# Sparse attention by gathered lists: first h gather tied to the 29th k|v row, degrees taken from records, later lists held, half of the h statistics beside the sort

## The chip, the cores and the metric

The kernel runs on one core of one Trainium2 chip. The metric is the device time of one execution in microseconds (us), lower is better. A core has TensorE (PE, with its weight loads shown apart as PEld), VectorE (DVE), ScalarE (ACT), GpSimd (POOL) and SyncE (SP). SP, ACT and POOL also start transfers, each through a queue of its own that works in order; the transfers all run on the same 16 DMA engines.

## The reference

One graph-attention layer over N = 4096 nodes with D = 512 features and 8 heads of 64. All masks that the inputs set are ones, and the layer norms' scales are ones and biases zeros.

```python
hs = layer_norm(x);  ht = layer_norm(h_target)
q = (ht @ Wq + bq) / sqrt(64);  k = hs @ Wk + bk;  v = hs @ Wv + bv
logits = einsum('thd,shd->hts', q, k);  logits = where(adj != 0, logits, -1e30)
ctx = einsum('hts,shd->thd', softmax(logits), v)
ht = layer_norm(ht + ctx @ Wo + bo)
out = layer_norm(x + ht + gelu(ht @ W1) @ W2)
```

`adj` is a 4096 x 4096 matrix of int32 (64 MB), symmetric with ones on the diagonal, in which about one element in 256 is set. So a node has some 17 neighbours, at most 39 in the tiles that the kernel provides for.

## The kernel before

The kernel doesn't compute the dense logits. It turns each row of `adj` into a list of its neighbours, sorts the nodes by degree, and gathers only the neighbours' k and v. A dense version of everything stands behind a flag for inputs that do not fit, and is not run here.

**Projections** (`project`, L859.). x is read in 16 groups of two tiles of 128 rows, normalized, transposed on PE, and multiplied by Wk and Wv. Each tile gives one "k|v row" of 128 x 1024 floats: `source` (L913) runs eight matmuls into PSUM (two halves of four), ACT copies each half to SBUF (L925), and ACT's queue stores the row to the DRAM table `kvd` (L927). There are 32 such rows. The SBUF buffer is `tq` (three of them) while h rows are still to be read, and then three slots of the ring.

**The ring** `kv` has 17 slots of 128 x 1024 floats. Slots 0 to 6 hold quarters of `adj` rows in the first stage, slot 7 small tables, slots 8 to 10 rows of h_target, slot 11 the first records, slots 12 to 16 groups of x. Afterwards the whole ring takes gathered k|v rows.

**Lists** (`edges`, L709). `adj` is read in 32 tiles of 128 rows, each in four quarters of 512 KB (`quarter`, L701). ACT takes the sign of a quarter and sums it for the degree (L721, three buffers `sg`). DVE multiplies the signs by positions and takes the largest eight of each of five segments (L726, L728). After four quarters DVE decodes and merges these into the 24 first neighbours, and the rest goes to DRAM (`rest_d`, L759). Tiles up to NA + FILL = 21 use the ring's slots; the later ones use two buffers `a`.

**h statistics** (`moments`, L793). Each of the 32 tiles of h_target is read by SP and gets a bn_stats and a bn_aggr on DVE. `edges` takes one after each odd quarter, so the 32 are done within the 16 tiles of part A. Then `prepare` (L1365) raises all 32 variances to -0.5 on POOL (L1372) and writes the results into both parts' records.

**Sort** (`sort`, L800). The lists of part A (16 tiles) are sorted by degree: counts by matmul with ones, a scan and a rank (L845), and 16 indirect scatters on POOL that write the records (degree, target, row, statistics, 24 neighbours) to DRAM (L848). `fill` makes FILL = 5 further list tiles beside it. Part B is sorted in the same way after all lists.

**Attention** (`attention`, L1121). Tiles are taken in an order that pairs large and small degrees. `prefetch` (L962) loads a tile's records (seven buffers `rec`; the first two by POOL, the others by SP). `front` (L975) gathers the tile's rows of h_target by index into a `tq` buffer (L958, issued by POOL), normalizes them on ACT (L984), transposes, and projects q (L997, L999). Each gather of k|v rows is an indirect DMA of 128 rows of 4 KB, issued by POOL (L958); gathers run four groups of up to three ahead. For each group DVE multiplies k by q and reduces (L1180, L1184), ACT takes the exponential, and DVE (L1143) and ACT (L1163) multiply v, which PE adds up by transposes (L1151). `finish` (L1038) divides by the sums, projects with Wo and normalizes.

**Feed-forward** (`feed`, L1276). Pairs of tiles run through W1, gelu and W2 (L1291, L1294, L1300), are normalized and scattered to the output (L1268).

**What orders the work.** Streams written as Python generators are woven by the costs that they yield (`_weave`); a scheduler then places instructions on the engines, in the order of its own estimates, each engine keeping that order on the chip. The first weave has the projections, `prepare` (lists, sort, first fronts) and `fill`; the second has attention, feed-forward and `other_lists`, which starts at 40 and yields 1.5 times the lists' costs, and ends with the sort of part B. `verdict` (L1215) checks that no degree is above the number of neighbours that its tile provides for; it loads the degrees from the sorted records with two strided DMAs (L1225).

Of the kernel before, what the change touches and what calls it, by code (L numbers as in the profile page):

```python
# [443 lines left out]
def adj_resnorm_kernel(  # L444
# [85 lines left out]
    with tc.tile_pool(name="keep", bufs=1) as keep:  # L530
# [17 lines left out]
        with ExitStack() as late:  # L548
            lp = late.enter_context(tc.tile_pool(name="lists", bufs=1))
            kp = late.enter_context(tc.tile_pool(name="kv", bufs=1))  # L550
            sp = late.enter_context(tc.tile_pool(name="s2", bufs=2))
            ps = late.enter_context(tc.tile_pool(name="ps", bufs=1, space=PSUM))
            src = ExitStack()
            kvw = src.enter_context(tc.tile_pool(name="kvw", bufs=1))
            wp2 = late.enter_context(tc.tile_pool(name="s2w", bufs=1, side="right"))
# [141 lines left out]
            adjs = []  # L697
            DEEP = 7
            FILL = 5

            def quarter(i, h):  # L701
                if i < NA + FILL:
                    a = ring[:, (i * NQ + h) % DEEP, :].bitcast(I32)
                else:
                    a = lp.tile([P, QW], I32, name="a", bufs=2)
                nc.sync.dma_start(a, adj[i * P:(i + 1) * P, h * QW:(h + 1) * QW])
                return a

            def edges(i):  # L709
# [4 lines left out]
                for h in range(NQ):  # L714
# [16 lines left out]
                    if h % 2 and moms:  # L731
                        moments(moms.pop(0))
# [126 lines left out]
            def project(order, t=None):  # L859
# [53 lines left out]
                def source(n, j):  # L913
                    g, hT = order[n], state[n][1]
                    if asked or moms:
                        kvr = sp.tile([P, 2 * D], F32, name="tq", bufs=3)
                    else:

                        kvr = ring[:, 8 + (n * G + j) % 3, :]
                    for half, w in enumerate((wk, wv)):  # L920
# [4 lines left out]
                        nc.scalar.copy(kvr[:, half * D:(half + 1) * D], pkv)  # L925
                    r0 = 1 + (g * G + j) * P
# [28 lines left out]
            recs, tqs, h2Ts, done, ready = {}, {}, {}, set(), []  # L955
# [19 lines left out]
            def front(i):  # L975
# [4 lines left out]
                t = tq[:, :D]  # L980
                gather(t, h_target, rec[:, TGT:TGT + 1])
# [56 lines left out]
            def finish(i, p, cps, group, hs, mv):  # L1038


                rec, tq, cap = recs[i], tqs.pop(i), TILES[i][1]
                pm = sp.tile([P, MAXE, H], F32, name="pm", bufs=1)
# [68 lines left out]
            def first_fronts():  # L1111

                for i in range(EARLY):
                    prefetch(i)
                for i in range(EARLY):
# [5 lines left out]
            def attention():  # L1121
# [47 lines left out]
                for group in GROUPS:  # L1169
# [3 lines left out]
                    for i in group:  # L1173
                        cps = ps.tile([P, KC, P], F32, name="cps", bufs=2)
                        while k < len(SG) and SG[k][0] == i:
# [7 lines left out]
                            lg = sp.tile([P, S, H], F32, name="lg")  # L1183
                            nc.vector.tensor_reduce(lg[:, :n, :],  # L1184
# [30 lines left out]
            def verdict():  # L1215
# [8 lines left out]
                for (i0, n), rec in zip(PARTS, recs_d):  # L1224
                    nc.sync.dma_start(degs[:, i0:i0 + n, :], rec.rearrange("(n p) w -> p n w", p=P)  # L1225
                                      [:, :, DEG:DEG + 1])
                for i, cap in enumerate(CAPS_A + CAPS_B):
# [136 lines left out]

            def prepare():  # L1365
# [3 lines left out]
                while moms:  # L1369
                    moments(moms.pop(0))  # L1370
                nc.vector.tensor_scalar_add(veh, mvh[:, :, 1], EPS)
                nc.gpsimd.tensor_tensor(rsh, veh, mhalf, ALU.pow)  # L1372
                nc.vector.scalar_tensor_tensor(nmh, mvh[:, :, 0], -1.0, rsh, op0=ALU.mult,
                                               op1=ALU.mult)
                for R, (i0, n) in zip(Rs, PARTS):
                    Rf = R.bitcast(F32)
                    nc.vector.tensor_copy(Rf[:, :, RST], rsh[:, i0:i0 + n])
                    nc.vector.tensor_copy(Rf[:, :, RST + 1], nmh[:, i0:i0 + n])
# [8 lines left out]
            def fill():  # L1387
# [3 lines left out]
                yield 9.0  # L1391
                for cost in _take(ed, FILL * steps):
                    yield cost

# [4 lines left out]
            s2wa = late.enter_context(tc.tile_pool(name="s2wa", bufs=1))  # L1399
            psf = late.enter_context(tc.tile_pool(name="psf", bufs=2, space=PSUM))  # L1400

            def other_lists():
                for cost in ed:
                    yield 1.5 * cost
# [38 lines left out]
```

## Time and profile before

| | |
|---|---|
| median of four runs | 1885.31 us (1879.07 to 1887.89) |
| profiled execution, its own time | 1885.55 us |
| span of that execution | 1883.8 us |
| mean granted TensorE clock | 0.957 |

Busy time by stage of that execution (us; the share is the mean over the 16 DMA engines):

| stage | PE | DVE | ACT | POOL | clock | DMA share |
|---|---|---|---|---|---|---|
| 0 to 250 | 226.92 | 212.99 | 165.84 | 25.03 | 0.97 | 0.97 |
| 250 to 360 | 58.69 | 78.26 | 49.66 | 51.94 | 0.77 | 0.77 |
| 360 to 650 | 263.30 | 262.01 | 212.45 | 143.03 | 0.96 | 0.76 |
| 650 to 700 | 39.99 | 20.84 | 21.98 | 35.16 | 0.83 | 0.53 |
| 700 to 1700 | 952.81 | 804.76 | 724.23 | 595.23 | 0.98 | 0.73 |
| 1700 to 1884 | 164.61 | 56.37 | 64.74 | 32.43 | 0.96 | 0.18 |

The first row is projections and lists, the second the sort of part A and the beginning of the attention, the third attention, feed-forward and the remaining lists, the fourth the sort of part B, the others attention and feed-forward alone. In a row of the instruction view stand the start, the duration, engine, line, operation, what is written and read, the count, and in brackets the idle time before it with what ended that. A busy PE can still be slowed by its clock. An idle engine costs something only where others wait for it.

### The profile page before, as it was taken

The numbers are of one execution on the slowest core, as the hardware profiler recorded it, in microseconds if no ns is written. First come the engines' busy times: TensorE is split into PE (matmuls) and PEld (weight loads), VectorE is DVE, ScalarE is ACT, GpSimd is POOL, SyncE is SP. The second block draws the span as 40 slices with busy tenths as digits, with TensorE's granted clock in tenths as the row PEclk, the third lists the DMA queues.
The fourth block names the chain that finished last, engine by engine and source line by source line (L and its number), as shares of the span: only waits on it lengthen the run. The fifth ranks groups of instructions, "written<-read, shape, count | busy, mean of one in ns | idle before, by whom it ended". The sixth has DMA issues, their size and how long they took to land. (4 is left out here: it accounts for less than half of the span.)

```text
span 1883.8 us, 22937 instructions
## 1 busy us (share of the span) xinstructions
PE 1706.3 (91%) x7030; PEld 1100.0 (58%) x7030; DVE 1435.2 (76%) x2595; ACT 1238.9 (66%) x3131; POOL 882.8 (47%) x804
## 2 busy tenths in 40 slices
PE   7989883688899989999999989999999999999995
PEld 3444431456566646766666656666666666666664
DVE  6989876899898737777878889889877768787400
ACT  5766644577786737776777767777767667777411
POOL 1000144545545465656666676655555545555101
PEclk9999996798999989999999999999999999999998
DMA  9999968978777646777778778767677767766000
GB/s 337 370 385 368 353 192 304 359 266 286 286 268 254 207 152 220 266 244 259 253 253 276 264 267 282 269 229 253 222 236 235 251 210 237 238 218 224 23 1 24
DMA packets 147757, 463.28 MB, mean 246 GB/s; under 512 B 24468, under 2 KB 29160, under 8 KB 147624
## 3 DMA queue, kind: packets, MB, share of 16 engines
q0 software_dynamic: 95696, 342.19, 53.4%
q1 hardware_dynamic: 45168, 98.54, 14.7%
q10 hardware_dynamic: 6760, 20.98, 2.8%
q8 instruction: 58, 0.95, 0.2%
q14 instruction: 75, 0.61, 0.1%
HBM read 430.76 MB, written 30.89 MB: 245 GB/s over the span
## 5 line engine op out<-in xcount | busy, mean ns | idle before, releaser
L958 POOL DMA_INDIRECT kv<-kvd,rec x603 | 685.1, 1136 | 523.2 <-PE cps L1151 240.9
L1291 PE MATMUL pf<-h2T,w 128*128 128x256 f32 (+1 forms) x2176 | 475.5, 370 | 5.1 <-issue 4.3
L1300 PE MATMUL po<-w,gt 128*128 128x512 f32 x1024 | 470.6, 601 | 0.0
L1180 DVE TENSOR_TENSOR kv<-kv,tq 128x1536 f32<-128x1536 f32 (+2 forms) x211 | 352.0, 1677 | 114.1 <-DMA kv<-kvd,rec 94.2
L1291 PEld LDWEIGHTS pf<-h2T,w 128*128 128x128 f32 x2176 | 390.4, 192 | 71.1 <-issue 26.2
L1163 ACT ACTIVATE kv<-kv,pa 128x64 f32<-128x64 f32 x1520 | 391.4, 336 | 4.6 <-ACT pa L1160 0.9
L1184 DVE TENSOR_REDUCE lg<-kv 128x24 f32<-128x1536 f32 (+2 forms) x211 | 350.6, 1669 | 2.4 <-ACT xt L1264 0.5
L1151 PE MATMUL cps<-ident,kv 128*128 128x128 f32 x2008 | 267.2, 281 | 61.3 <-DVE kv L1143 38.7
L1151 PEld LDWEIGHTS cps<-ident,kv 128*128 128x128 f32 x2008 | 239.6, 145 | 137.2 <-issue 61.1
L1300 PEld LDWEIGHTS po<-w,gt 128*128 128x128 f32 x1024 | 188.7, 194 | 190.0 <-issue 189.4
L1143 DVE TENSOR_TENSOR kv<-kv,p 128x1024 f32<-128x1024 f32 (+1 forms) x211 | 249.6, 1191 | 46.5 <-ACT p L1188 37.8
L681 POOL TENSOR_TENSOR n_rs<-n_ve,mhalf 128x2 f32<-128x2 f32 (+1 forms) x50 | 43.3, 867 | 323.8 <-DVE n_ve L674 152.1
L1294 ACT ACT_TABLE_LOAD x108 | 138.6, 1283 | 1.6
L923 PE MATMUL pq<-wk,h2T 128*128 128x512 f32 x256 | 125.2, 634 | 11.0 <-ACT h2T L908 5.9
L728 DVE MAX8 cand<-sg 128x8 uint16<-128x103 uint16 (+1 forms) x640 | 131.5, 253 | 1.8 <-DVE gid L749 0.8
L721 ACT ACTIVATE sg<-kv 128x1024 uint8<-128x1024 int32 x84 | 88.7, 1058 | 65.3 <-DMA kv<-in_adj_dram 34.8
L1294 ACT ACTIVATE gt<-pf 128x512 f32<-128x512 f32 x128 | 76.4, 597 | 80.0 <-PE pf L1291 63.3
L997 PE MATMUL t<-wq,tq 128*128 128x512 f32 x256 | 117.9, 603 | 10.6 <-ACT tq L991 8.3
L923 PE MATMUL pq<-wv,h2T 128*128 128x512 f32 x256 | 117.7, 602 | 4.8 <-ACT kv L925 3.0
L1073 PE MATMUL t<-wo,rb 128*128 128x512 f32 x256 | 120.0, 613 | 1.4 <-DVE rb L1063 1.4
L1188 ACT ACTIVATE p<-lg 128x24 f32<-128x24 f32 (+2 forms) x179 | 33.6, 188 | 91.8 <-DVE lg L1184 64.5
L923 PEld LDWEIGHTS pq<-wk,h2T 128*128 128x128 f32 x256 | 50.6, 205 | 72.8 <-issue 54.9
(171 smaller groups left out, 1607.9 us busy)
## 6 DMA issues: line engine op xcount, KB each, us to landing
kv<-in_adj_dram SPq DMA_DIRECT2D x84, 512.0 KB
a<-in_adj_dram SPq DMA_DIRECT2D x44, 512.0 KB
kvd<-tq ACTq DMA_DIRECT2D x24, 512.0 KB
kv<-kvd,rec POOLq DMA_INDIRECT x603
kv<-in_L_gnn_h_target_dram SPq DMA_DIRECT2D x32, 256.0 KB
kv<-in_x_dram SPq DMA_DIRECT2D x15, 512.0 KB
w<-in_L_gnn_W_dram SPq DMA_DIRECT2D x6, 1024.0 KB
rest_d<-gid SPq DMA_DIRECT2D x32, 160.0 KB
```

The lines of the kernel that those rows point to most:

```text
L728: nc.vector.max(cand[:, h * SQ + s, :], wd[:, w0:w1])
L923: nc.tensor.matmul(pkv, hT[:, kc, j * P:(j + 1) * P], w[:, kc, :], start=kc == 0, stop=kc == KC - 1)
L958: nc.gpsimd.indirect_dma_start(out=dst, out_offset=None, in_=table[:, :], in_offset=bass.IndirectOffsetOnAxis(ap=idx, axis=0))
L1073: nc.tensor.matmul(pa, ct[:, c, :], wo[:, c, :], start=False, stop=c == KC - 1, skip_group_check=True)
L1143: nc.vector.tensor_tensor(v4, v4, p[:, j0:j0 + m, :].unsqueeze(3) .to_broadcast([P, m, H, HD]), ALU.mult)
L1151: nc.tensor.matmul(cps[:, c, :], kv[:, j, D + c * P:D + (c + 1) * P], ident, is_transpose=True, start=j0 + j == 0 and c == 0, stop=j0 + n ...
L1163: nc.scalar.mul(v, v, pa[:, hd:hd + 1])
L1180: nc.vector.tensor_tensor(kv[:, :n, :D], kv[:, :n, :D], tq[:, :D].unsqueeze(1).to_broadcast([P, n, D]), ALU.mult)
L1184: nc.vector.tensor_reduce(lg[:, :n, :], kv[:, :n, :D].rearrange("p j (h d) -> p j h d", h=H), AX.X, ALU.add)
L1291: nc.tensor.matmul(pf[:, k, :], w1[(f0 + k) // KC][:, kc, (f0 + k) % KC * P:((f0 + k) % KC + 1) * P], h2T[:, kc, :w], start=kc == 0, stop= ...
L1294: nc.scalar.activation(gt, pf, AF.Gelu_apprx_tanh)
L1300: nc.tensor.matmul(po[j], gt[:, k, j * P:(j + 1) * P], w2[(f0 + k) // KC][:, (f0 + k) % KC, :], start=False, stop=f0 + k == FC - 1, skip_g ...
```

## The change

- *h statistics.* In the first 16 list tiles one statistic is taken per tile (after the second quarter), from the 17th on three. `norms(part)` raises the 16 variances of one part and writes them to its records; part A's stands before the sort, part B's at the end of `fill`. FILL is 6 instead of 5, and `fill` begins at 6 instead of 9.
- *k|v rows.* The rows of the first 14 groups go through `tq`; the last four go through ring slots 13 to 15 instead of 8 to 10, which still hold h.
- *First h gather.* The first fronts are begun in the order of the weave only after the 29th k|v row; a one-column copy on ACT from that row into the gather's destination makes the gather wait for it.
- *Later lists.* The first two adjacency quarters into `a` that are asked for once a group's logits exist get a one-column copy on ACT from the newest logits first, and so wait for them.
- *Degrees.* `finish` copies the degree of its tile from the record in SBUF with one POOL instruction; the two loads from DRAM go. The check then compares in the tiles' order.
- *Pace.* `other_lists` yields 2.0 times the lists' costs.
- The pool stack `late` is renamed `last`; `late` is now the list that holds the 29th row.

```diff
@@ quarter, edges
             else:
                 a = lp.tile([P, QW], I32, name="a", bufs=2)
+                if logits and len(held_back) < 2:
+                    held_back.append(i)
+                    nc.scalar.copy(a.bitcast(F32)[:, 0:1], logits[-1])
             nc.sync.dma_start(a, adj[i * P:(i + 1) * P, h * QW:(h + 1) * QW])
...
-                    if h % 2 and moms:
+                    if (h == 1 or i >= NA and h != 2) and moms:
                         moments(moms.pop(0))
...
-            FILL = 5
+            FILL = 6
@@ source
-                    if asked or moms:
+                    if n < NG - 2:
                         kvr = sp.tile([P, 2 * D], F32, name="tq", bufs=3)
                     else:
-                        kvr = ring[:, 8 + (n * G + j) % 3, :]
+                        kvr = ring[:, 13 + (n * G + j) % 3, :]
...
+                    if n == 14 and j == 0:
+                        late.append(kvr)
@@ front, finish, first_fronts
                 t = tq[:, :D]
+                if i < EARLY:
+                    nc.scalar.copy(t[:, 0:1], late[0][:, 0:1])
                 gather(t, h_target, rec[:, TGT:TGT + 1])
...
                 rec, tq, cap = recs[i], tqs.pop(i), TILES[i][1]
+                nc.gpsimd.tensor_copy(degs[:, i, :], rec[:, DEG:DEG + 1])
...
                     prefetch(i)
+                while not late:
+                    yield None
@@ attention, verdict
                             lg = sp.tile([P, S, H], F32, name="lg")
+                            logits[:] = [lg[:, 0, 0:1]]
...
-                for (i0, n), rec in zip(PARTS, recs_d):
-                    nc.sync.dma_start(degs[:, i0:i0 + n, :], rec.rearrange("(n p) w -> p n w", p=P)
-                                      [:, :, DEG:DEG + 1])
-                for i, cap in enumerate(CAPS_A + CAPS_B):
+                for i, (_, cap) in enumerate(TILES):
@@ prepare, fill, other_lists
+            def norms(part):
+                i0, n = PARTS[part]
+                while moms and moms[0] < i0 + n:
+                    moments(moms.pop(0))
+                me = slice(i0, i0 + n)
+                nc.vector.tensor_scalar_add(veh[:, me], mvh[:, me, 1], EPS)
+                nc.gpsimd.tensor_tensor(rsh[:, me], veh[:, me], mhalf[:, me], ALU.pow)
+                nc.vector.scalar_tensor_tensor(nmh[:, me], mvh[:, me, 0], -1.0, rsh[:, me],
+                                               op0=ALU.mult, op1=ALU.mult)
+                Rf = Rs[part].bitcast(F32)
+                nc.vector.tensor_copy(Rf[:, :, RST], rsh[:, me])
+                nc.vector.tensor_copy(Rf[:, :, RST + 1], nmh[:, me])
...
                 ready.append("lists")
-                while moms:
-                    moments(moms.pop(0))
-                nc.vector.tensor_scalar_add(veh, mvh[:, :, 1], EPS)
-                nc.gpsimd.tensor_tensor(rsh, veh, mhalf, ALU.pow)
...
+                norms(0)
...
-                yield 9.0
+                yield 6.0
                 for cost in _take(ed, FILL * steps):
                     yield cost
+                norms(1)
...
-                    yield 1.5 * cost
+                    yield 2.0 * cost
```

## The prediction

> **What bounds the kernel now.** I read four views in this order: the busy times of the engines, the windows by stage, the instructions in order of time on POOL, ACT and DVE around the two places where the windows show PE idle, and the DMA queues of one such place.
>
> The busy times say that PE has the least slack, DVE the next least:
>
> ```profile
> PE 1706.3 (91%) x7030; PEld 1100.0 (58%) x7030; DVE 1435.2 (76%) x2595; ACT 1238.9 (66%) x3131; POOL 882.8 (47%) x804
> ```
>
> PE is idle for 1883.8 - 1706.3 = 177.5 us. The windows show where (window, then PE, PE loads, DVE, ACT, POOL busy us, granted clock, DMA share, GB/s):
>
> ```profile
> 200.00:250.00 50.00, 44.40 (x117) 20.44 (x116) 42.30 (x180) 31.08 (x59) 10.78 (x7) 0.93 0.91 341
> 250.00:300.00 50.00, 37.92 (x93) 16.86 (x92) 31.48 (x130) 25.12 (x49) 17.30 (x19) 0.93 0.54 161
> 300.00:320.00 20.00, 2.59 (x7) 0.80 (x5) 11.37 (x38) 6.26 (x14) 11.86 (x12) 0.67 0.88 324
> 320.00:340.00 20.00, 5.64 (x24) 4.84 (x24) 17.02 (x25) 8.96 (x35) 12.63 (x9) 0.50 1.03 406
> 340.00:360.00 20.00, 12.54 (x58) 9.52 (x59) 18.39 (x19) 9.32 (x36) 10.14 (x10) 0.72 0.96 381
> 650.00:700.00 50.00, 39.99 (x147) 23.87 (x146) 20.84 (x22) 21.98 (x57) 35.16 (x34) 0.83 0.53 161
> ```
>
> Between 250 and 360 PE loses 12.1 + 17.4 + 14.4 + 7.5 = 51.4 us, between 650 and 700 another 10.0. From 700 to 1700 PE is 95% busy. From 360 to 650 it loses 27 of 290 us while DVE is 90% busy: there the remaining lists and the attention share DVE. So the change is worth what it does in the hand-over from projections to attention, in the lists-beside-attention stage, and at the second sort near 650.
>
> The hand-over on POOL (last scatter, first and last early gather, first k|v gather), then on ACT:
>
> ```profile
> 263.38 0.99 POOL L848 DMA_INDIRECT rec<-kv,ranki  x1 [0.31 <-issue]
> 269.42 1.02 POOL L958 DMA_INDIRECT tq<-in_L_gnn_h_target_dram,rec  x1 [2.11 <-DMA rec<-rec]
> 274.80 0.94 POOL L958 DMA_INDIRECT xt<-in_x_dram,rec  x1 [0.30 <-issue]
> 304.15 0.94 POOL L958 DMA_INDIRECT kv<-kvd,rec  x1 [28.41 <-DMA a<-in_adj_dram]
> ```
>
> ```profile
> 262.79 1.06 ACT L721 ACTIVATE sg<-kv 128x1024 uint8<-128x1024 int32 x1 [7.17 <-issue]
> ...
> 273.00 0.81 ACT L984 ACTIVATE tq<-tq,rec 128x512 f32<-128x512 f32 x1 [4.08 <-DMA tq<-in_L_gnn_h_target_dram,rec]
> ...
> 283.20 1.06 ACT L721 ACTIVATE sg<-a 128x1024 uint8<-128x1024 int32 x1 [3.99 <-DMA a<-in_adj_dram]
> ...
> 295.38 1.06 ACT L721 ACTIVATE sg<-a 128x1024 uint8<-128x1024 int32 x1 [2.00 <-DMA a<-in_adj_dram]
> ...
> 297.03 0.33 ACTq L927 DMA_DIRECT2D kvd<-kv  x1
> ```
>
> The reader is to see that the k|v gathers wait 28.4 us on POOL, and that the 32nd k|v row is stored at 297.03 only because ACT, which works in order, stood 7.2 us ("issue" in the row; in the program that sign waits for DVE to free its buffer), 4.1 us for the first h gather and 6 us for adjacency quarters with copies of finished rows behind. And on DVE a pause ahead of the sort, the first product and a starved one at the second sort:
>
> ```profile
> 208.68 0.19 DVE L1373 SCALAR_TENSOR_TENSOR kv<-kv 128x32 f32<-128x32 f32 x1 [5.55 <-POOL kv L1372]
> ...
> 315.54 1.76 DVE L1180 TENSOR_TENSOR kv<-kv,tq 128x1536 f32<-128x1536 f32 x1 [5.54 <-DMA kv<-kvd,rec]
> ...
> 688.73 1.76 DVE L1180 TENSOR_TENSOR kv<-kv,tq 128x1536 f32<-128x1536 f32 x1 [13.62 <-DMA kv<-kvd,rec]
> ```
>
> **The change part by part.** The sum is made against the profiled execution's own 1885.55 us (span 1883.8), which stands 0.2 us above the median of the four runs, 1885.31. Positions come from the order in which the two programs' instructions stand on each engine.
>
> *Half of the h statistics beside the sort.* Two statistics take 1.28 us and their two aggregates 0.30 (rows at 209.10 and 210.29), so 0.79 each. Ahead of the degree sum (212.1) 14 of them go: 11.1 us. The power pause halves: POOL took 5.43 us for 32 columns and 0.58 for one, so 16 take about 2.9, minus 2.6. If DVE alone set the time the degree sum would come 13.7 us sooner; but ACT waits 18 us for adjacency quarters between 100 and 250, and its order ties the lists to PE's rows, of which only one fewer stands ahead (two halves of 3.43 and its share of transposes, 7.4 us). I take the mean, 10.6. Between degree sum and ranks the new order puts 8 statistics (6.3), two more quarters (1.3 each) and one more list end (3.8): plus 12.7. So the ranks come about 2 us later than 243.7; between 1 us sooner and 5 later by these two readings.
>
> *POOL behind the scatters.* The 16 scatters (20.3 us) stay. Ahead of the first h gather now stand both x gathers (2 x 1.25) and three copies of a degree. No copy on POOL is in the trace; I bound it by DVE's smallest, 0.17, and POOL's one-column power, 0.58, and take 0.58, the same engine: 1.7. The third copy also waits for a record that SP loads, 3.3 us of issue after the scatters, which the x gathers cover. With the ranks' 2 us the h gather starts at 275.6 instead of 269.4. The tie to the 29th row adds nothing: that row's first half was copied at 254, before any record. The second power (2.9) stands ahead of the k|v gathers, but DVE asks for it near 280, well before 295. All 32 copies are at most 18.6 us on an engine that is idle for 1001 us, so they are no term by their length. The Trainium skill, page "GPSIMD Engine Reference", section 3.1, speaks against putting them there: elementwise work on that engine costs about twice DVE's time. An estimate from that page and DVE's 0.17 would be 32 x 0.34 = 10.9 us, less than the bound by the row, and the sum would be the same.
>
> *The last rows.* In ACT's order the scale that waits for the h gather still stands ahead of the 30th row's copy, which moves from 273.7 to about 280. But from there to the last store ACT has only three signs of quarters (seven before), all of quarters loaded before the scatters, so the 3.99 + 0.74 + 0.56 + 2.00 us of waits for adjacency go. From 280: the 30th row is whole at 285, both halves of the 31st at 287, PE needs 3.6 us for each half of the 32nd (5.8 at the low clock, as 288.87 shows). The store comes at 294.8, minus 2 us. Bounds: minus 12, if DVE's slow stretch from 252 to 268 (8 us busy of 16) does not come back; plus 5, if the ranks are 5 late and the last waits stay.
>
> *Later lists held.* From the first k|v gather to the first product pass 11.4 us, with four quarters (2 MB) in flight. Without them the nearest row is the h gather, 3.6 us from start to use; the third gather starts 3.5 us after the first; with double the bytes I allow 4, together 7.5, minus 4 us (bounds 0 and minus 4). Held back are four quarters and one list end, 4 x 1.25 + 3.8 = 8.8 us of DVE. By the 41st product (593 us before) both orders have done the same list work since the first product, so the 8.8 us fall after 600, where DVE has 29 us free between 650 and 700 and 12 in the next 50: cost 0, at most 8.8 if that cover is gone. The four one-column copies that ACT gains for the tie and the hold cost 0.17 each, as its gate of the last weights does. What SP has queued behind a held quarter: later quarters, the writes of rest and the later records; DVE's lists wait for the first, nobody early for the others.
>
> *Lists at 2.0 instead of 1.5.* The 27 us that PE loses from 360 to 650 shrink with less list work per time; 10 lists over a third more time. I take minus 2 (0 to minus 8, about a third of 27).
>
> *The second sort.* Its 16 scatters stood almost in a row: no k|v gather from 662.8 to 684.5, and DVE starved 13.6 us. Now 8 scatters run, then k|v gathers stand between the rest: the longest gap is about 10 us, so DVE's wait should fall to 2 or 3. PE lost 10 us in that window, and part of it is slow issue from 678 to 694 that follows scatters in both orders. I take minus 5 (minus 10 to plus 3).
>
> *Degrees from records.* Two loads go from SP. In the DMA queues from 252 to 268 the first is the bulk of this row:
>
> ```profile
> q1 hardware_dynamic: 2087, 0.01, 7.4%
> ```
>
> 7.4% of 16 us is 1.2 us of DMA, while the engines were otherwise nearly idle; SP waits for the scatters with the records anyway. I take 0. The Trainium skill, page "DMA: Bandwidth & Descriptors", Rules for kernel authors, says that a strided last dimension becomes one descriptor per element, which the packet count agrees with; a rule for a gain, which this row prices at 1 us at best.
>
> Sum: -2 - 4 + 0 - 2 - 5 + 0 = -13, so 1885.55 - 13 = 1872.5, said as 1872.
>
> **The rivals.**
> 1. Slower: a degree copy holds POOL. 25 copies stand between k|v gathers, and each waits for a record that SP loads behind adjacency quarters; four of these kept SP from 411 to 468, 14 us each. Between an out scatter, which frees the record's place, and its copy POOL has 8 gathers, 10 us. A record 14 us late holds POOL about 4 us, for each of the 8 tiles whose lists are still open; PE and DVE then starve as at 688. From the fourth such hold on it eats the 13 us; five or six, 20 to 24 us, end at 1892 to 1896. Against it: records 7 to 9 were issued within 5 us of their out scatter.
> 2. No change: PE makes up nothing, because after 360 it is bound by DVE and the held 8.8 us come back: -13 + 8.8 + 2 for the pacing is -2, 1883 (1880 to 1888).
> 3. More: the ranks come early (the 13.7 us in full) and DVE's slow stretch misses ACT. Last store near 285: -12 - 4 - 4 - 8 = -28 at most, 1857; I put it at 1862. For it: DMA ran at 0.99 to 1.02 between 50 and 200, and 14 h rows, 3.7 MB, leave that stretch.
>
> **How the numbers follow.** Forecast 0.42 (1866 to 1879), rival 3 0.20, rival 2 0.17, rival 1 0.21. A measurement of this kernel tells about 0.3%, 5.7 us, from no change. Faster: 0.42 and 0.20; rival 2 is mostly within: 0.16; slower 0.22. The range goes from 1856, rival 3's end, to 1893, at the lower part of rival 1, and leaves out about 0.15.
>
> **What would show it.** Right: first k|v gather near 302, first product near 309, no quarter landing between them, the DVE wait near the second sort under 5 us, PE loss from 250 to 360 about 45 us. Wrong: POOL idle ahead of a degree copy for several us; the h gather past 280; DVE over 95% busy with PE idle after 650; or a first product after 315.

## The result and the profile after

The changed kernel takes 1891.1 us (median of 48 runs, 1881.6 to 1897.3) against 1885.7 us for the kernel before (75 runs, 1878.2 to 1891.2): the ratio is 1.0028, with a 95% interval of 1.0021 to 1.0035. The forecast was 1872 us, so the change went the other way, by 5 us up instead of 13 down.

The profiled execution of the changed kernel took 1887.6 us (span 1885.7), 2.05 us more than that of the kernel before. The busy times of the engines:

```profile
PE 1704.4 (90%) x7030; PEld 1103.0 (58%) x7030; DVE 1433.7 (76%) x2597; ACT 1225.7 (65%) x3127; POOL 886.7 (47%) x837
```

PE, DVE and ACT are busy less in all than before (by 1.9, 1.5 and 13.2 us), POOL with its 32 copies 3.9 us more. What changed is where PE waits. The windows by stage of the kernel before (columns as in the prediction: window, then PE, PE loads, DVE, ACT, POOL busy us, granted clock, DMA share, GB/s):

```profile
0.00:250.00 250.00, 226.92 (x593) 106.05 (x594) 212.99 (x907) 165.84 (x304) 25.03 (x40) 0.97 0.97 361
250.00:360.00 110.00, 58.69 (x180) 32.02 (x179) 78.26 (x209) 49.66 (x132) 51.94 (x49) 0.77 0.77 275
360.00:650.00 290.00, 263.30 (x1236) 181.91 (x1235) 262.01 (x513) 212.45 (x558) 143.03 (x129) 0.96 0.76 264
650.00:900.00 250.00, 238.12 (x1073) 161.81 (x1072) 171.59 (x170) 163.29 (x437) 151.19 (x140) 0.97 0.70 231
900.00:1400.00 500.00, 469.69 (x2063) 318.79 (x2062) 417.89 (x426) 366.48 (x998) 313.02 (x268) 0.97 0.75 254
```

The same windows of the changed kernel:

```profile
0.00:250.00 250.00, 223.11 (x594) 103.86 (x595) 217.31 (x926) 167.96 (x311) 24.02 (x41) 0.98 0.99 365
250.00:360.00 110.00, 67.42 (x218) 39.30 (x217) 69.47 (x169) 46.95 (x138) 62.26 (x64) 0.77 0.70 256
360.00:650.00 290.00, 259.56 (x1185) 177.86 (x1185) 260.25 (x530) 211.48 (x546) 131.61 (x124) 0.95 0.76 267
650.00:900.00 250.00, 227.77 (x1020) 156.79 (x1019) 165.27 (x167) 147.90 (x406) 148.32 (x139) 0.95 0.64 217
900.00:1400.00 500.00, 476.04 (x2120) 324.82 (x2119) 426.77 (x433) 373.83 (x1024) 316.69 (x284) 0.99 0.77 261
```

The idle time of PE is the window's length less its first busy figure:

| stage | PE idle before, us | after | difference | the prediction's steps |
|---|---|---|---|---|
| 0 to 250 | 23.1 | 26.9 | +3.8 | none |
| 250 to 360 | 51.3 | 42.6 | -8.7 | -2 (last rows) and -4 (hold) |
| 360 to 650 | 26.7 | 30.4 | +3.7 | -2 (pace), 0 (deferred work) |
| 650 to 900 | 11.9 | 22.2 | +10.3 | -5 (second sort) |
| 900 to 1400 | 30.3 | 24.0 | -6.3 | none |

The hand-over came out as well as foreseen, or better. In the instructions of POOL in order of time, the first k|v gather starts at 294.12 instead of 304.15:

```profile
294.12 1.03 POOL L964 DMA_INDIRECT kv<-kvd,rec  x1 [17.34 <-DMA kvd<-kv]
```

In those of DVE, the first product starts at 303.30 instead of 315.54:

```profile
303.30 1.76 DVE L1192 TENSOR_TENSOR kv<-kv,tq 128x1536 f32<-128x1536 f32 x1 [4.07 <-DMA kv<-kvd,rec]
```

Followed gather by gather (the first is number 0, so that n gathers stand ahead of the n-th), the lead is spent early. The 20th k|v gather starts 15 us sooner than before (322.8 against 338.2), the 40th 9 us, the 60th 4, the 80th 4 later (489.2 against 485.3). From there to the 140th it swings between 4 us sooner and 6 later. Then comes the second sort. In the kernel before its 16 scatters ran from 656 to 679; here, on POOL, they run from 722.90 to 758.87. First, last and one in the middle:

```profile
722.90 1.02 POOL L852 DMA_INDIRECT rec<-R,ranki  x1 [0.30 <-issue]
...
744.32 1.72 POOL L852 DMA_INDIRECT rec<-R,ranki  x1 [0.30 <-issue]
...
758.87 1.01 POOL L852 DMA_INDIRECT rec<-R,ranki  x1 [0.30 <-issue]
```

DVE, in order of time, waits for k|v gathers beside them in two pieces, and once more near 870:

```profile
743.39 1.76 DVE L1192 TENSOR_TENSOR kv<-kv,tq 128x1536 f32<-128x1536 f32 x1 [5.06 <-DMA kv<-kvd,rec]
761.58 1.76 DVE L1192 TENSOR_TENSOR kv<-kv,tq 128x1536 f32<-128x1536 f32 x1 [8.88 <-DMA kv<-kvd,rec]
...
870.89 0.69 DVE L1192 TENSOR_TENSOR kv<-kv,tq 128x512 f32<-128x512 f32 x1 [6.61 <-DMA kv<-kvd,rec]
```

The kernel before has, behind its one wait of 13.62 us, a second one:

```profile
700.81 1.76 DVE L1180 TENSOR_TENSOR kv<-kv,tq 128x1536 f32<-128x1536 f32 x1 [6.05 <-DMA kv<-kvd,rec]
```

DVE's waits of over 3 us for k|v gathers in this stage come to 20.6 us here and to 19.7 there, so they are not the difference. PE now has two long pauses; the kernel before has none of over 2 us in this stage, and loses its 10 us at the sort in many short ones:

```profile
769.99 1.12 PE L997 MATMUL t<-ident,tq 128*128 128x128 f32 x4 [8.36 <-ACT h L1087]
880.76 6.32 PE L1006 MATMUL t<-wq,tq 128*128 128x512 f32 x8 [8.63 <-issue]
```

The first pause follows the scatters, the second comes some 110 us behind the last of them. In windows of 50 us, the kernel before:

```profile
850.00:900.00 50.00, 48.57 (x235) 34.04 (x234) 36.50 (x36) 34.09 (x93) 35.59 (x31) 1.00 0.77 267
```

The changed kernel:

```profile
700.00:750.00 50.00, 47.38 (x212) 32.83 (x211) 35.00 (x42) 26.55 (x75) 32.75 (x30) 0.97 0.52 169
750.00:800.00 50.00, 41.01 (x184) 28.02 (x182) 30.79 (x30) 26.79 (x80) 34.77 (x32) 0.90 0.67 223
850.00:900.00 50.00, 41.37 (x179) 28.13 (x178) 28.65 (x30) 26.63 (x72) 30.50 (x29) 0.90 0.66 231
```

So at the sort PE loses 9.0 us (11.6 with the 50 us ahead), where the kernel before lost 10.0 from 650 to 700. Another 8.6 go from 850 to 900, where the kernel before lost 1.4.

The 220th gather is 6 us late, as the 140th was, with one sort behind both kernels. The 240th, behind the second pause, is 17 us late (917.9 against 900.5); the stage from 900 to 1400 gives that back by the 380th (1196.1 against 1196.2). The last gather is 2 us late, and so is the end.

### The profile page after: what moved, and what is told of

Its sections match the earlier page's. It is cut to its first block, busy times and chain, and to the rows that moved or that the text cites. A ratio compares the mean times of both kernels' runs of the same rounds, so it can differ in the third digit from the quotient of the medians.

```text
span 1885.7 us, 23007 instructions
## 1 busy us (share of the span) xinstructions
PE 1704.4 (90%) x7030; PEld 1103.0 (58%) x7030; DVE 1433.7 (76%) x2597; ACT 1225.7 (65%) x3127; POOL 886.7 (47%) x837
## 3 DMA queue, kind: packets, MB, share of 16 engines
q1 hardware_dynamic: 41040, 98.52, 14.6%
## 5 line engine op out<-in xcount | busy, mean ns | idle before, releaser
L1163 PE MATMUL cps<-ident,kv 128*128 128x128 f32 x2008 | 267.7, 281 | 40.5 <-DVE kv L1155 29.2
L1155 DVE TENSOR_TENSOR kv<-kv,p 128x1024 f32<-128x1024 f32 (+1 forms) x211 | 249.7, 1191 | 44.9 <-ACT p L1201 40.7
L681 POOL TENSOR_TENSOR n_rs<-n_ve,mhalf 128x2 f32<-128x2 f32 (+1 forms) x50 | 38.0, 759 | 321.3 <-DVE n_ve L674 172.3
L1006 PE MATMUL t<-wq,tq 128*128 128x512 f32 x256 | 125.8, 637 | 26.5 <-ACT tq L1000 16.4
L725 ACT ACTIVATE sg<-kv 128x1024 uint8<-128x1024 int32 x88 | 93.0, 1060 | 74.4 <-DVE cand L732 34.8
L927 PE MATMUL pq<-wk,h2T 128*128 128x512 f32 x256 | 121.3, 616 | 9.8 <-ACT h2T L912 5.5
L1006 PEld LDWEIGHTS t<-wq,tq 128*128 128x128 f32 x256 | 50.8, 204 | 86.1 <-issue 64.4
```

Of the source, the lines that this page charges most:

```text
L927: nc.tensor.matmul(pkv, hT[:, kc, j * P:(j + 1) * P], w[:, kc, :], start=kc == 0, stop=kc == KC - 1)
L1006: nc.tensor.matmul(pq, hT[:, kc, :], wq[:, kc, :], start=kc == 0, stop=kc == KC - 1)
L1155: nc.vector.tensor_tensor(v4, v4, p[:, j0:j0 + m, :].unsqueeze(3) .to_broadcast([P, m, H, HD]), ALU.mult)
L1163: nc.tensor.matmul(cps[:, c, :], kv[:, j, D + c * P:D + (c + 1) * P], ident, is_transpose=True, start=j0 + j == 0 and c == 0, stop=j0 + n ...
```

## The experiments

Three theories were set against each other at first. P: the pace of 2.0 does the harm, through the place of the second sort. C: the degree copies hold POOL. H: the held list work gives back the gain of the hand-over. The parts other than pace, hold and copies (half of the statistics beside the sort, six lists beside the projections instead of five, the tie, the ring places) are called the hand-over's parts below.

All results in one table. "Place" is the number of k|v gathers that stand on POOL, in the order of the program, ahead of the second sort's first scatter; PE idle is from the windows of each profiled execution.

| run | parts of the change in it | place | PE idle 360 to 900, us | ratio to before (95%) |
|---|---|---|---|---|
| before | none | 142 | 38.6 | 1 |
| after | all | 165 | 52.7 | 1.0028 (1.0021 to 1.0035) |
| e1 | all, pace 1.5 | 127 | 53.9 | 1.0035 (1.0016 to 1.0054) |
| e2 | all but the hold | 165 | 49.0 | 1.0021 (1.0003 to 1.0039) |
| e11 | the same again | 165 | 44.7 | 1.0016 (0.9994 to 1.0038) |
| e3 | all but the copies | 165 | 52.3 | 1.0027 (1.0012 to 1.0042) |
| e4 | hand-over | 127 | 40.5 | 0.9983 (0.9968 to 0.9997) |
| e16 | the same again | 127 | 39.8 | 0.9984 (0.9968 to 1.0001) |
| e5 | hand-over, hold | 127 | 50.9 | 1.0033 (1.0016 to 1.0050) |
| e6 | hand-over, pace 2.0 | 165 | 45.9 | 0.9984 (0.9966 to 1.0002) |
| e12 | the same again | 165 | 48.4 | 1.0007 (0.9992 to 1.0023) |
| e7 | hand-over, copies | 127 | 39.9 | 0.9995 (0.9979 to 1.0010) |
| e8 | hand-over, short hold, pace 1.83 | 127 | 43.4 | 1.0009 (0.9986 to 1.0032) |
| e9 | hold alone on the kernel before | 142 | 43.7 | 0.9998 (0.9984 to 1.0012) |
| e10 | hand-over, hold, eight lists | 108 | 42.4 | 1.0021 (1.0004 to 1.0037) |
| e13 | all, scatters in two blocks | 165 | 53.6 | 1.0028 (1.0013 to 1.0043) |
| e14 | hand-over, hold, five lists | 142 | 46.4 | 1.0008 (0.9991 to 1.0024) |
| e15 | hand-over, hold, pace 1.65 | 141 | 46.2 | 0.9991 (0.9972 to 1.0010) |
| e17 | all, pace 1.65 | 141 | 44.9 | 0.9994 (0.9975 to 1.0013) |
| e18 | hand-over, pace 1.65 | 141 | 38.2 | 1.0011 (0.9995 to 1.0027) |

**Pace, hold and copies, each undone; the hand-over alone.** The edits of the changed kernel in e1, e2 and e3 (e4 makes all three):

```diff
 # e1: other_lists
-                    yield 2.0 * cost
+                    yield 1.5 * cost
 # e2: quarter
-                    if logits and len(held_back) < 2:
-                        held_back.append(i)
-                        nc.scalar.copy(a.bitcast(F32)[:, 0:1], logits[-1])
 # e3: finish
-                nc.gpsimd.tensor_copy(degs[:, i, :], rec[:, DEG:DEG + 1])
 # e3: verdict
+                for (i0, n), rec in zip(PARTS, recs_d):
+                    nc.sync.dma_start(degs[:, i0:i0 + n, :], rec.rearrange("(n p) w -> p n w", p=P)
+                                      [:, :, DEG:DEG + 1])
-                for i, (_, cap) in enumerate(TILES):
+                for i, cap in enumerate(CAPS_A + CAPS_B):
```

> The changed kernel with one number undone: the later lists yield 1.5 times their cost again instead of 2.0. On POOL the second sort's first scatter then follows the 127th k|v gather instead of the 165th (142nd in the kernel before). Theory P (the pace does the harm: the trace of the changed kernel loses 10 us more on PE between 650 and 900 than the kernel before, around a second sort at 723 to 759): the sort is back near 620 to 660, PE loses about 2 us between 700 and 900 instead of 20, and the time falls by 10, to about 1881. Theory C (the degree copies hold POOL between the gathers): the copies are all still there, so the time stays near 1891. Theory H (the held lists give back the hand-over's gain between 360 and 500): the hold is still there and the work comes denser, so it stays at 1891 or rises a little.

> The changed kernel without the hold: the two one-column copies that tie the first later quarters to the second tile's logits are gone, so those quarters are loaded as soon as their buffers are free. The order of instructions on POOL is the same. Theory H: the lead of 15 us at the 20th k|v gather is no longer spent on late lists, the lead at the 80th gather stays near 10 instead of minus 4, and the time falls by about 8.8, the DVE time that was deferred, to 1882. Theories P and C: four quarters in flight at the hand-over make the first product some 4 us later, nothing else moves, and the time is between 1891 and 1895.

> The changed kernel with the degrees loaded by two transfers at the end, as in the kernel before, and no copies of a degree on POOL. Theory C: the 25 holds of POOL between k|v gathers are gone; PE loses about 10 us less between 700 and 900 (8.6 of them ahead of 880), the time falls to about 1881. Theories P and H: POOL has 32 copies of 0.2 us less, nobody waited for them; 1891 within 2.

> The kernel before with the hand-over's parts alone: half of the h statistics beside the sort, six lists beside the projections, the first h gather tied to the 29th k|v row, other ring places; no hold, pace 1.5, degrees loaded at the end. The second sort's scatters stand behind the 127th k|v gather. All theories have the first k|v gather near 294 as in the changed kernel (304 in the kernel before). Theory P: the gain of the hand-over, about 5 us of PE time before 360, is kept: 1880 to 1882. Theory C and theory H: the same, as both suspects are absent. If it stays within 2 us of the kernel before, the hand-over's gain is lost by itself, since PE between 360 and 650 is bound by something else, and neither of the three holds.

No part undone by itself gave the 5 us back: 1.0035 without the pace, 1.0021 without the hold, 1.0027 without the copies. Theory C falls with e3 at once: 1.0027 against 1.0028. Theory P in its first form falls with e1: PE idle between 700 and 900 did fall from 20 us to 0.2, but 15.6 us appeared between 650 and 700 (2.0 in the changed kernel) and 27.5 between 360 and 500 (17.6). The hand-over alone is faster than both kernels, but not by its own hand-over: what all theories expected of it, a first gather near 294, missed. In e4 it starts about where it did in the kernel before (304.15), on POOL:

```profile
306.31 1.00 POOL L960 DMA_INDIRECT kv<-kvd,rec  x1 [29.34 <-DMA kvd<-kv]
```

The reason stands on ACT in the same run. Without the hold, signs of later quarters stand between the copies of the last rows, and wait for DVE and for quarters:

```profile
285.43 1.06 ACT L721 ACTIVATE sg<-a 128x1024 uint8<-128x1024 int32 x1 [3.02 <-DMA a<-in_adj_dram]
...
295.86 1.06 ACT L721 ACTIVATE sg<-a 128x1024 uint8<-128x1024 int32 x1 [1.43 <-DVE cand L728]
...
298.01 1.06 ACT L721 ACTIVATE sg<-a 128x1024 uint8<-128x1024 int32 x1 [1.01 <-DMA a<-in_adj_dram]
...
299.67 0.33 ACTq L929 DMA_DIRECT2D kvd<-kv  x1
```

With the hold these signs are gone from there, and the last store comes at 291.24 in the changed kernel and 290.03 in e5. So it is the hold that moves the hand-over, and not only by keeping the DMA free for the first gathers, as the prediction had it.

**Each part alone on the hand-over.** e5 is e1 with e3's edit, e6 is e2 with e3's, e7 is e1 with e2's. e8 is e5 with a shorter hold and another start and pace of the later lists:

```diff
-                        nc.scalar.copy(a.bitcast(F32)[:, 0:1], logits[-1])
+                        nc.scalar.copy(a.bitcast(F32)[:, 0:1], late[1][:, D:D + 1])
-                    if n == 14 and j == 0:
+                    if (n, j) in ((14, 0), (15, 1)):
-            WAIT = 40.0
+            WAIT = 0.0
-                    yield 1.5 * cost
+                    yield 1.83 * cost
```

> The hand-over's parts with the hold of the later lists, pace 1.5, degrees loaded at the end: against the kernel of the hand-over alone (0.9983 of the kernel before) only the hold is added. Theory H (the hold gains 11 us at the first k|v gather and then pays more than that, since about 11 us of DVE work leave a stretch where DVE waits, 275 to 306, for one where it is the bound, 340 to 610): first gather near 295, the 120th near 610 instead of 594, PE between 360 and 500 at 112 us busy instead of 123, time near 1892 (1.0035 of before), all of the loss of the run with pace 1.5. Theory C (the degree copies are what cost there): 1881 to 1884.

> The hand-over's parts with pace 2.0, no hold, degrees loaded at the end: only the pace is added to the hand-over alone. Theory P (the pace costs, through the place of the second sort behind the 165th gather): PE idle between 700 and 900 near 20 us instead of 2, and some 13 us less of it between 600 and 700; time near 1888 (1.002 of before), 7 us above the hand-over alone. Theory C: the pace alone costs nothing, 1881.

> The hand-over's parts with the degree copies on POOL, pace 1.5, no hold: only the copies are added to the hand-over alone. Theory C: 1888 to 1892, with POOL idle ahead of a copy between k|v gathers. Theories H and P: 1880 to 1882, the same as the hand-over alone.

> The hand-over's parts with the two held quarters tied to the last k|v row instead of the second tile's logits; the other lists start at once (no wait of 40 units) at 1.83 times their cost, which leaves the second sort behind the 127th gather; degrees loaded at the end. On ACT five signs then stand right behind the last k|v store, ahead of the first products. Theory H: the first gather keeps its 295, and the list work goes back to the stretch in which DVE waits for the first gathers, so the 11 us are kept in part: 40th gather near 390, time 1872 to 1878 (0.993 to 0.996). If the loss of the hold does not come from the deferred list work but from later quarters landing among the k|v gathers, the time is near that of the hold alone, 1890.

The hold on the hand-over costs half a per cent (1.0033 against 0.9983 and 0.9984, intervals apart). What the traces show beside it: by 340 us, 100.4 quarters of lists had their candidates taken by DVE in e4 (five maxima each, counted in the trace), 96.4 in the kernel before, 90.0 in e5 and in the changed kernel. (The expectations further down have counts that are 0.6 to 2.0 lower.) At 1.25 us a quarter and 3.8 a list end, e5 defers, by estimate, 10.4 x 1.25 + 2.6 x 3.8 = 23 us of DVE work against e4. Its first gather is 13 us sooner, its 120th 16 us later (610.4 against 594.3). The pace alone and the copies alone move nothing beyond their intervals. e8, in which 96.0 quarters were done by 340 us, had the first gather at 293.0 and still ended at 1.0009: below e5, with intervals that overlap, and no gain over e4. Its expected 0.993 to 0.996 is missed.

**Is it the hold by itself?** e9 puts the hold's lines of e2, and the line that fills `logits`, into the kernel before; e10 is e5 with `FILL = 8`. e11 and e12 repeat e2 and e6 side by side on one chip.

> The kernel before with the hold of the later lists alone; everything else, the second sort's place included, stays. Theory H (the hold moves list work out of the stretch where DVE waits for the first k|v gathers into the one where DVE is the bound: at 340 us 88.6 quarters are done with it in the run that added it to the hand-over, 99.8 without): the first gather comes 10 us or more before 304, quarters done at 340 fall from 94.4 to about 83 to 85, the 120th gather is 10 or more late against 596, and the time rises by 0.3 to 0.6%, to 1.003 to 1.006 of the kernel before. If the hold costs only together with the hand-over's other parts, the ratio is 0.998 to 1.001.

> The hand-over's parts with the hold at pace 1.5 and degrees loaded at the end, as in the run of the hold alone (1.0033), but with eight lists beside the projections instead of six, so that two lists (eight quarters) less are left when the hold begins. Theory H: the loss follows the quarters done at 340 us, 0 at 99.8 quarters (0.9983), 0.26% at 95.2 (1.0009), 0.5% at 88.6 (1.0033); with the two lists more, about 96 quarters are done and the ratio comes down to 1.000 or below, unless the ranks, and with them the first gather, come so much later that the gain of the hand-over goes. If the loss is in the hold itself (the gate's place on ACT and SP, the burst of quarters at 332), the ratio stays near 1.003.

> Once more the kernel with the hand-over's parts, pace 2.0 and the degree copies on POOL, without the hold (1.0021 on another chip), beside the same kernel without the copies on this chip. If the copies cost what those two runs differed by, this one is 0.3 to 0.4% above its neighbour. If that was the difference of two chips, they agree within 0.15%.

> Once more the hand-over's parts with pace 2.0, no hold and no degree copies (0.9984 on another chip), as the neighbour of the run with the copies. 0.997 to 1.000 of the kernel before in either theory.

e9 speaks against theory H as it stood. On the kernel before, the hold brings the first gather to 289.7, defers 9.4 quarters of work (87.0 done at 340 instead of 96.4), has lost the whole lead of 14 us at the 120th gather (596.3 in both), and ends level: 0.9998. In its trace most gathers from the 130th on are 3 to 5 us sooner than before, but that execution is 5.1 us under the median of its run. By the median the lead is lost, but nothing more than the lead. e10 has 98.0 quarters done at 340 and still ends at 1.0021, above e8 with 96.0 and the kernel before with 96.4, so the loss does not follow that number alone (its first gather, at 298.55, is also 5 us later than that of e5). e11 and e12 differ by 0.1%, in the direction of a price for the copies, well inside both intervals. And e12 is the same program as e6: 0.9984 on one chip, 1.0007 on another. A single comparison of this kind is good to about 0.2%.

**The place of the second sort.** What e9 has in common with the kernel before, and e5, e1 and the changed kernel do not, is the place of the second sort behind the 142nd gather. e13 keeps the place of the changed kernel and takes the gaps between the scatters; e14 and e15 bring the place back in e5, by two different ways:

```diff
 # e13, on the changed kernel: sort
-                    yield 1.3
+                    yield 0.0 if part else 1.3
 # e14, on e5
-            FILL = 6
+            FILL = 5
 # e15, on e5
-                    yield 1.5 * cost
+                    yield 1.65 * cost
```

> The changed kernel whole, but the second sort's scatters yield nothing, so eight of them follow the 165th gather and the other eight the 168th, instead of 8, 1, 2, 4 and 1 up to the 175th. If the spread scatters starve the attention longer than a block would (722.9 to 758.9 in the changed kernel against 656 to 679 in the kernel before, with PE 8.4 us idle at 762), the loss of PE between 700 and 800 falls from 12 to about 6 and the time by 5, to 1886. If the place behind the 165th gather costs it, whatever the spacing, 1890 to 1892.

> The run of the hold on the hand-over's parts (1.0033) with five lists beside the projections instead of six; the second sort's scatters then follow the 142nd and 144th gather as in the kernel before, and eleven lists are left. If the sort's place is what makes the hold cost more here than on the kernel before, the ratio falls to 0.999 to 1.001. If the split statistics, the tie or the ring places do it, it stays at 1.003; and if only the quarters done at 340 counted, it would rise above 1.004, since one list less is done.

> The same run of the hold on the hand-over's parts with pace 1.65 instead of 1.5 and six lists, which brings the second sort behind the 141st and 144th gather by the pace. If the sort's place does it: 0.999 to 1.001, as with five lists. If it was the number of lists beside the projections: 1.003 here, and 1.000 with five lists.

> Once more the hand-over's parts alone (0.9983 on another chip). If it is a kernel faster than the one before, 0.997 to 0.9995; if the first value was the chip's, 0.9995 to 1.001.

The spacing of the scatters is not the cause (1.0028 as before the edit; PE idle from 650 to 900 even 23.9). The place fits: with it back, e14 and e15 end at 1.0008 and 0.9991 instead of 1.0033, two ways of bringing it back; the interval of e15 is apart from that of e5, that of e14 overlaps with it. e13, e14 and e15 ran on the same chip. e16 repeats e4's gain. The last two runs put the question to the change itself: the changed kernel with `yield 1.65 * cost` (e17), and e4 with the same line (e18).

> The changed kernel with one number changed: the later lists at 1.65 times their cost instead of 2.0, which brings the second sort's scatters from behind the 165th to 175th gather to behind the 141st to 144th. If the sort's place makes the change slower: PE idle from 650 to 900 falls from 22 to 11 to 13 us as in the three runs with the hold and that place, and the ratio is 0.999 to 1.001 instead of 1.0028. If the degree copies or the hold itself make it slower: 1.0025 to 1.0035.

> The hand-over's parts alone, without hold and degree copies, with pace 1.65: the second sort behind the 141st to 144th gather instead of the 127th to 135th. If that place is better by itself, PE idle from 650 to 900 falls from 14 to 11 to 13 and the ratio from 0.9983 to 0.997. If the place matters only with the hold, because there the lists end about 20 us later against the gathers, 0.998 to 0.999 as at the 127th.

e17 is the whole change with one number different, and it is no slower than the kernel before: 0.9994, against 1.0028, with intervals that do not touch (the upper end 1.0013, the lower 1.0021). It ran on the chip of e1 and e3, which had 1.0035 and 1.0027. The window of the stage in e17:

```profile
650.00:900.00 250.00, 240.12 (x1109) 166.82 (x1108) 179.17 (x177) 172.54 (x461) 159.16 (x148) 0.98 0.70 237
```

The same window in e13:

```profile
650.00:900.00 250.00, 226.06 (x1014) 156.00 (x1013) 163.92 (x168) 146.36 (x400) 147.80 (x139) 0.95 0.64 216
```

PE is idle 9.9 us in e17, 23.9 in e13 and 22.2 in the changed kernel. In e17 the scatters run almost in a row, from 658.12 to 682.69, and DVE waits 11.71 us for a k|v gather right behind them; as this row of its DVE shows:

```profile
683.08 1.76 DVE L1192 TENSOR_TENSOR kv<-kv,tq 128x1536 f32<-128x1536 f32 x1 [11.71 <-DMA kv<-kvd,rec]
```

PE has only one pause of over 2 us in the whole stage:

```profile
701.01 5.76 PE L1310 MATMUL po<-w,gt 128*128 128x512 f32 x8 [9.26 <-ACT gt L1304]
```

From 850 to 900 it loses nothing, where the seven runs with pace 2.0 lose 6.0 to 8.8 us and the others at most 1.9. Around the sort itself, from 5 us ahead of the first scatter to 75 behind it, PE loses 9.9 us in e17, 9.1 in the changed kernel and 10.0 in the kernel before. So in the changed kernel the place doesn't work through a longer pause at the sort.

Two things limit the finding. First, e18: without the hold, that place also gives 11.2 us of PE idle from 650 to 900, yet the run ends at 1.0011, above the 127th place (0.9983, 0.9984), where at most 0.999 was expected; and e6 and e12 lose 20.2 and 22.1 us in that stage and end at 0.9984 and 1.0007. So the place decides together with the hold, and not by itself, and idle time in that stage alone doesn't make a run slower. Second, no run moves the sort and nothing else: 1.65 instead of 2.0 also makes the lists denser. That it is the place and not the pace rests on e9 and e14, which have pace 1.5 and the 142nd place and end at 0.9998 and 1.0008, where e5, with pace 1.5 and the 127th, ends at 1.0033; and these two have five lists beside the projections where e5 has six. The end of the lists (the last sign starts at 557 us in e16, 572 in e18 and in the kernel before, 575 to 577 in e5, e15 and e17, 612 in the changed kernel) doesn't order the runs either.

## Why the prediction was wrong, by its own steps

*The second sort, minus 5.* This is the step that failed. It took the price of the sort in the kernel before (10 us of PE) as given, and asked only how the spread of the scatters would lower it. The spread did not lower it: PE loses 9.0 us at the sort, and the time without the spread is the same (e13). The change also moves the sort, from behind the 142nd gather to behind the 165th, and with it the order of what follows; the prediction gives that no price. From 650 to 900 PE idle went from 11.9 to 22.2, plus 10.3 instead of minus 5, of which 7.2 are the second pause, near 880, that no step had. With the one number of the pace changed that brings the sort to behind the 141st gather, the whole deficit is gone (e17). DVE's wait was forecast at 2 to 3 us; it was 5.06 and 8.88.

*Lists at 2.0, minus 2.* It was meant to relieve DVE from 360 to 650. PE idle there rose by 3.7. This step is also what displaced the sort; the two should have been one step. Part of it comes back from 900 to 1400, which no step had either: PE is idle there 24.0 to 28.0 us in the seven runs with pace 2.0 (27.8 in e8 with 1.83), 30.3 in the kernel before and 30.7 to 35.5 in the others with pace 1.5 or 1.65; so pace alone, on the hand-over, costs nothing that two runs could settle (0.9984, 1.0007).

*Later lists held, minus 4, and the deferred 8.8 us at cost 0.* The size of the deferred work was about right and the cover was wrong. By 360 us DVE had run 204.3 us of the instructions of `edges` against 214.5 in the kernel before, 10.2 us less. From the first gather to the first product 9.2 us passed, where 11.4 passed before and 7.5 were forecast, so 2.2 of the 4 us came. (One row was misread there: in the kernel before the third gather starts 2.5 us after the first and ends 3.4 after it; 3.5 was taken for the start.) The first product still came at 303.3, sooner than the 309 forecast, because the first gather did. But the deferred work was not absorbed after 600 for nothing: the lead was gone by the 80th gather, at 489 us, and in e9, where nothing else changes, by the 120th. Rival 2 named this mechanism ("the held 8.8 us come back") and put it at no change, which is what e9, with the hold alone, measured (0.9998).

*The last rows, minus 2.* The store came at 291.24 rather than 294.8, and the first gather at 294.12 rather than 302. But the step gave this to the new order of rows and statistics; e4 has those and no gain (306.31), e9 has the hold alone and all of it (289.7). The right waits were named, signs of quarters between the copies of rows, and they were put down to the wrong part of the change.

*Half of the statistics beside the sort.* The first scatter started at 242.2 instead of 244.1, where 2 us later was taken and 1 us sooner was the bound. What it did to PE before 250 was left out: idle there is 23.6 to 27.1 us in every run with the hand-over's parts, 23.1 in the kernel before and 21.9 in e9.

*POOL behind the scatters, and the degrees.* The h gather started at 270.08, not 275.6. A copy was taken at 0.58 us; the 32 copies have a median of 0.198 us, nearer to DVE's 0.17. Rival 1, that a copy would hold POOL behind a late record, did not happen: POOL stood idle 3.9 us in all, three times, ahead of a copy. The Trainium skill, page "GPSIMD Engine Reference", section 3.1, which the prediction used, measures its factor of two on an add with two inputs; section 4.1 says that operations with one input run there at roughly line rate. A copy of one column is too short to test a rate, but at 0.198 beside 0.17 it is not twice DVE's time. The two loads that went were 4128 packets of the queue in the prediction (45168 before, 41040 after); putting them back (e3) moved nothing, 1.0027 against 1.0028. The term of 0 was right within what the runs can tell: the five other comparisons with and without the copies (e1 and e5, e2 and e6, e7 and e4, e11 and e12, e17 and e15) range from plus 0.02% to plus 0.37%. All point to a small price, but only e11 and e12, 0.09% apart, ran on one chip.

*What stays open.* The stages' differences in PE idle time explain the profiled pair, 2.05 us apart. The medians are 5.4 us apart, and a profiled execution can lie further from the median of its run than that (9.4 us above in e1, 8.1 below in e11). The six runs with 49.0 us or more of PE idle time from 360 to 900 all end at 1.0021 to 1.0035, but below that the sum does not order the runs: e18 has less of it than e16, and is slower, and e10 ends at 1.0021 with 42.4. Why the 142nd place is right with the hold and the 127th without was not settled; no run tells its reason.

The best version found is the hand-over alone, without hold, copies and pace: 0.9983 (0.9968 to 0.9997) and 0.9984 (0.9968 to 1.0001), about 3 us under the kernel before and at the edge of what these intervals tell from no change.

## What to carry to other kernels

When a change alters how fast one stream of work is woven into another, price every step that this moves, above all a burst on a queue that the other stream needs, and what then stands behind it: here the burst's own pause cost about the same at both places, its spacing nothing, and a new pause stood some 110 us further on. An early start is worth only what the next bound stage does not take back, so follow a milestone through the whole run (here the n-th gather) before counting it. And undo several parts together as well as singly: here no single undoing showed the cause, because the hold was free at one place of the sort and cost half a per cent at another.

## What the runs showed of the hardware

Two executions of one and the same program (e6 and e12, on two chips) had spans of 1876.5 and 1890.4 us, with 7030 matmuls each, PE busy 1696.4 and 1703.7 us and a mean granted clock of 0.963 and 0.957. They agree to about 3 us up to the 200th k|v gather (817.6 and 820.7) and drift apart by 14 us up to the last (1730.9 and 1744.8). A difference of 10 us between two single profiles of this kernel says nothing without its stage.
